# Four heads in one query tile, and projections two heads further ahead, in an attention and mixture-of-experts kernel

## The chip, the cores and the metric

The kernel runs on one core of a Trainium2 chip. The metric is the time of one execution on the device in microseconds (us); lower is better. The median of five runs is given for the kernel before, and one more execution was taken with the hardware profiler. PE is TensorE (matmul), PEld its weight load, DVE is VectorE, ACT ScalarE, POOL GpSimd, SP SyncE, which issues most DMAs. A name with q behind it (SPq) is the queue of that engine.

## What is computed

The input x is 4 sequences of 512 tokens with 256 features, all in float32. Reduced to what matters:

```python
xn = layernorm(x)                                  # over 256 features
q, k, v = xn @ Wq, xn @ Wk, xn @ Wv                # 16 query heads, 4 key/value heads, 128 wide
q, k = rotate(q) * xs, rotate(k) / xs              # rotary embedding with a position scale
s = softmax(causal(q @ k.T / sqrt(128))) @ v @ Wo  # query heads 4m .. 4m+3 share k and v head m
y = sum over the 2 best of 16 experts of weight * (silu(xn @ Wg) * (xn @ Wu)) @ Wd
y = y + (silu(xn @ Sg) * (xn @ Su)) @ Sd           # the shared expert, 352 wide
out = x + s * silu(y)
```

Causal means that query token t sees only the keys of tokens 0 to t of its sequence.

## The kernel before

There are G = 64 heads in all: 4 sequences of 16. One loop (L1038) runs over steps g, and each step works on several heads at different stages: it projects head g (`project`, L709), makes the scores and the exponentials of head g-2 (`score`, L734; `exponents`, L761), turns the probabilities of head g-3 (`turned`, `sent`, `brought`, L807 to L831), multiplies those of head g-4 by the values (`weigh`, L833), and makes a quarter of an output projection for the group of four heads that ended two groups ago (`output`, L857). The order on PE, DVE, ACT and SP is the order in which the program is written (`manual_schedule`, L1025); POOL's order is left to the tool that schedules the program.

**Projection.** A head is two matmuls of 128x128 weights with 512 tokens (L690) into a PSUM tile `pr` (two buffers). ACT copies the two halves crosswise (L698, L699), DVE multiplies and adds (L702, L704, L706). With every fourth head comes a key head, projected in the same way, in the step where g % 4 is 0. Each head has a tile qT of its own, with three buffers.

**Scores.** A query tile is 128 consecutive tokens of one head, so a head has four, i = 0 to 3. Tile i needs the first (i+1)*128 keys: one matmul of 128, 256, 384 or 512 columns (L753). DVE adds the mask and finds the maximum (L756), ACT takes the exponential and sums (L766). The four results stand side by side in a tile `prob` of 1280 columns (two buffers), and `normalise` (L777) multiplies by 1/sum on ACT (L783).

**Turning.** The weighted sum needs the probabilities transposed. For heads below GT = 61, DVE transposes blocks of 32x32 in five instructions (`turned`, L814). `sent` writes the result to DRAM with four DMAs on SP's queue (pt_d, L827), and `brought` reads it back in another order (pT, L831). SP works through its queue in order and waits in it. The last three heads are transposed by TensorE.

**Weighing and output.** `weigh` (L847) makes four matmuls of 512, 384, 256 and 128 columns into `po`, and ACT copies the result into a tile oT (L853). `output` multiplies a token tile of four heads by Wo (L863) and adds to s_sb.

**Plain steps.** `plain(g)` (L655) names steps with little beside attention. In them `output` comes ahead of `weigh` and `normalise` stands ahead of both; in other steps the order is `weigh`, `normalise`, `output`. PSUM banks of scores are also chosen by it.

**Everything else** is put at named places of steps (`put`, L920, six places in each step: START, SCORED, TURNED, PROJECTED, WEIGHED, END): the value projections (`value`, steps 0 to 2 for the first sequence and 6 to 10 for the others), the shared expert (`shared_hidden`, L567, three pieces of eight matmul passes for each sequence; `shared_down`), the router (steps 6 to 18), the scatter of tokens into blocks by indirect DMAs on POOL (steps 16 to 23, four in each), 40 blocks of expert work (steps 24 to 46: `block_load` with a copy `wb` on POOL, `block_hidden`, `block_down`), gathers and the final gate (from step 46). The statistics of later sequences are made by ACT (`stats_of`, L264) and POOL (`stats_of_last`, L278), and POOL normalises them (L300). DMAs in the list `later` are issued once a step, just after `brought`: among them clearing xs_d and ys_d (L178), weights, and from step 52 on writing s_d and reading it back (sr, L634).

Of the kernel before, what the change touches and what calls it, by code (L numbers as in the profile page):

```python
# [12 lines left out]
F32 = mybir.dt.float32  # L13
# [15 lines left out]
def kernel(  # L29
# [14 lines left out]
):  # L44

# [127 lines left out]
    nc.sync.dma_start(rp[:, :2], rope[:2].rearrange("k p s -> p k s"))  # L173
    for b in range(1, B):
        nc.sync.dma_start(xn[:, ts(b, NQ), :], xf[:, ts(b, NQ), :])
# [6 lines left out]

    def load_rest():
        nc.sync.dma_start(sgu, sh_gate_up.rearrange("(c p) j -> p c j", p=P))
        load_wq(1)
# [25 lines left out]
    )  # L211
    eps_t = const.tile([P, 1], F32, name="eps_t")
# [124 lines left out]
    both = rt.tile(full, F32, name="r_both")  # L337
# [52 lines left out]
    def route_slots():  # L390

        nc.gpsimd.tensor_sub(pos, run, both)

        cn = ps_s.tile([P, 2, E], F32, name="s")
        nc.tensor.matmul(cn[:, 0, :], before, run[:, NT - 1, :], start=True, stop=True)
        nc.tensor.matmul(cn[:, 1, :], ones, run[:, NT - 1, :], start=True, stop=True)
        cnt = rt.tile([P, 2, E], F32, name="r_cnt")
        nc.scalar.copy(cnt, cn)
        yield

        sq = [P, E, NT]
        cmp = rt.tile(sq, F32, name="r_cmp")
        nc.vector.tensor_tensor(
            cmp, cnt[:, 1, :].unsqueeze(2).to_broadcast(sq),
            steps.unsqueeze(1).to_broadcast(sq), ALU.is_gt,
        )
        nb = rt.tile([P, E], F32, name="r_nb")
        nc.vector.tensor_reduce(nb, cmp, AX.X, ALU.add)
        yield
        cum = rt.tile([P, E, E], F32, name="r_cum")  # L410
        nc.vector.tensor_tensor(
            cum, nb.unsqueeze(1).to_broadcast([P, E, E]), upto, ALU.mult
        )
        end = rt.tile([P, E], F32, name="r_end")
        nc.vector.tensor_reduce(end, cum, AX.X, ALU.add)
        yield
        base = rt.tile([P, E], F32, name="r_base")
        nc.vector.tensor_sub(base, end, nb)
        nc.vector.scalar_tensor_tensor(
            base, base, float(P), cnt[:, 0, :], ALU.mult, ALU.add  # L420
        )
        nc.gpsimd.tensor_tensor(pos, pos, base.unsqueeze(1).to_broadcast(full), ALU.add)
        for k in range(K):
            nc.gpsimd.tensor_mul(pick[k], pick[k], pos)
        yield
        sf = rt.tile([P, K, NT], F32, name="r_sf")
        for k in range(K):
            nc.vector.tensor_reduce(sf[:, k, :], pick[k], AX.X, ALU.add)
        nc.vector.tensor_copy(slot, sf)
        yield  # L430

        wide = [1, NB, E]
        le = rt.tile(wide, F32, name="r_le")
        nc.vector.tensor_tensor(
            le, iota_b.unsqueeze(2).to_broadcast(wide),
            end[0:1, :].unsqueeze(1).to_broadcast(wide), ALU.is_ge,
        )
        yield
        ex = rt.tile([1, NB], F32, name="r_ex")
        nc.vector.tensor_reduce(ex, le, AX.X, ALU.add)  # L440
        nc.vector.tensor_scalar_min(ex, ex, float(E - 1))
        nc.vector.tensor_copy(blk[:, :NB], ex)
        nc.vector.tensor_copy(blk[:, NB:], end[0:1, E - 1 :])
# [28 lines left out]
    def block_xs(i, n):  # L472

        xs = fe.tile([P, 2, D], F32, name="xs")
        nc.sync.dma_start(xs[:, :n, :], xs_d[i * P : (i + n) * P, :].rearrange("(n p) d -> p n d", p=P))
        for k in range(n):
            xsT_t[i + k] = xs[:, k, :]

    def block_load(i, copy=nc.gpsimd.tensor_copy):
# [7 lines left out]
        wb = fe.tile([P, NC, 2 * IB], F32, name="wb", bufs=3)  # L487
# [44 lines left out]
    def block_down(i, n):  # L532
# [5 lines left out]
        if not ys_t:  # L538
            ys_t.append([fe.tile([P, 2, D], F32, name="ys"), 0])
# [27 lines left out]
    def shared_hidden(b, c):  # L567

        if c == 0:
            hsT_t[b] = w2.tile([P, NS, S], F32, name="hsT")  # L570
# [83 lines left out]

    def plain(g):  # L655


        return g % GRP and (ROUTED <= g < E0 or E1 + 2 * NS <= g < GT + 2)

# [26 lines left out]
    def rotated(b, w, h, cs, sn, name, bufs):  # L686
# [14 lines left out]
        r = w2.tile([P, S], F32, name=name, bufs=bufs)  # L701
# [4 lines left out]
        nc.vector.tensor_add(r, pr, t2)  # L706
        yield r

    def project(g):  # L709

        b, h = divmod(g, NH)
        if h % GRP == 0:
            for kT[b, h // GRP] in rotated(b, wk, h // GRP, 2, 3, "kT", 2):
                yield
        for qT[g] in rotated(b, wq, h, 0, 1, "qT", 3):
            yield
# [16 lines left out]

    def score(g, i):  # L734


        b, h = divmod(g, NH)
        if i == 0:
            last = g == G - 1
            pb = w2.tile([P, off[NQ]], F32, name="turned" if last else "prob", bufs=2)  # L740
            mx = small.tile([P, NQ], F32, name="mx")
            prob[g] = (pb, mx)
        pb, mx = prob[g]
        w = (i + 1) * P
# [5 lines left out]
        elif i == NQ - 1 and g < GT and not E0 < g + 2 < E1:  # L750
# [3 lines left out]
            sc[:, :w], qT[g][:, ts(i, P)], kT[b, h // GRP][:, :w], start=True, stop=True  # L754
        )
        nc.vector.tensor_tensor_reduce(  # L756
            pb[:, off[i] : off[i + 1]], sc[:, :w], mask[:, S - w :],
# [3 lines left out]
    def exponents(g, i):  # L761
# [3 lines left out]
        pi = pb[:, off[i] : off[i + 1]]  # L765
# [11 lines left out]
    def normalise(g, i):  # L777
# [3 lines left out]
        pi = pb[:, off[i] : off[i + 1]]  # L781
# [51 lines left out]
    def weigh(g):  # L833
# [16 lines left out]
        oT[g] = w2.tile([P, S], F32, name="oT", bufs=2 * GRP)  # L850
        if g < GT:
            po = po.rearrange("p (a i q) -> p i a q", a=QB, q=32)
            paced.append(nc.scalar.copy(oT[g].rearrange("p (i a q) -> p i a q", a=QB, q=32), po))  # L853
        else:
            paced.append(nc.scalar.copy(oT[g], po))

    def output(q, t, pool=ps_s, name="s"):  # L857
# [4 lines left out]
        for j in range(GRP):  # L862
            nc.tensor.matmul(  # L863
                s, oT[q * GRP + j][:, ts(t, P)], wo[:, k * GRP + j, :],
# [13 lines left out]
    def ending(j, t):  # L878

        h = NH - GRP + j  # L880
        if j == 0:
# [3 lines left out]
            end_t[t], oT[G - GRP + j][:, ts(t, P)], wo[:, h, :],  # L885
# [10 lines left out]
    def weigh_last():  # L896
# [5 lines left out]
        oT[g] = w2.tile([P, S], F32, name="oT", bufs=2 * GRP)  # L902
        for t in range(NQ + 1):
            if t < NQ:
# [6 lines left out]
                nc.scalar.copy(oT[g][:, ts(t, P)], po[:, ts(t, P)])  # L911
# [15 lines left out]
    ROUTED = NH - 1  # L927

    put(0, TURNED, router_weights)
    put(0, PROJECTED, value, 0, 0, PO, PS)  # L930
    put(1, PROJECTED, value, 0, 1, TP, TP)
    put(1, PROJECTED, value, 0, 2, PO, PS)
    put(2, PROJECTED, value, 0, 3, TP, TP)

    put(0, START, stats_of_last)
    for n, g in enumerate((0, 0, 0, 0, 1, 1, 2, 3)):
# [13 lines left out]
    for g, f in (  # L950
        (4, partial(load_wo, 0)), (5, partial(load_wq, 2)), (8, partial(load_wo, 1)), (9, partial(load_wq, 3)),
# [10 lines left out]
    for g, p in (  # L962
        (13, PROJECTED), (14, TURNED), (14, TURNED), (15, TURNED), (16, TURNED), (17, TURNED), (18, TURNED)
# [22 lines left out]
    for i in range(1, NB0, 2):  # L986
        g = E0 + 1 + i // 2
        put(g, WEIGHED, block_hidden, i, *(PR if g % GRP else TP))

    for b in range(B):  # L990
        S0 = (3, 12)[b] if b < B // 2 else E1 + NS * (b - B // 2)
        S1 = ROUTED + NQ + 2 * b if b < B // 2 else S0 + NS
# [32 lines left out]
    with tc.manual_schedule(engines={ET.PE, ET.DVE, ET.Activation, ET.SP}):  # L1025
# [11 lines left out]
        load_rest()  # L1037
        for g in range(G + GRP):  # L1038
# [7 lines left out]
            pieces = project(g) if g < G else iter(())  # L1046
# [29 lines left out]
            for _ in range(1 if g % GRP else 2):  # L1076
# [85 lines left out]
```

## Time and profile before

| | us |
|---|---|
| median of 5 runs (743.87 to 746.73) | 745.44 |
| the profiled execution | 747.31 |
| its span, first to last instruction | 745.6 |
| DVE, transposes L814 (x305) | 106.3 |
| ACT, exponentials L766 (x252) | 140.2 |
| ACT, normalise L783 (x246) | 118.4 |
| PE, projections L690 (queries, x256) | 121.2 |
| PE, weigh L847 (x504) | 147.4 |
| PE, output L863 (x472) | 111.7 |

The span is what lies between the first and the last instruction; the execution's own time is 1.7 us longer. Busy times of an engine are sums over its instructions. Those of PE overlap, as a matmul is still in the pipeline when the next one starts, so the means of single matmuls are longer than the distance between two starts. DMAs moved 154.87 MB, a mean of 208 GB/s; the 61 reads pT have a median of 4.4 us from issue to landing, the 244 writes pt_d 2.8 us. An "x" behind a group is its count.

### The profile page before, as it was taken

What the parts mean: (1) busy time and instruction counts of PE and PEld (TensorE: products, weight loads), DVE (VectorE), ACT (ScalarE), POOL (GpSimd) and SP (SyncE); (2) the same over time, 40 slices, a digit from 0 to 9 for tenths busy, and PEclk for the clock granted to TensorE, in tenths of its full rate; (3) what the DMA queues carried; (4) which work ended last, traced back from release to release, by engine and by line L of the source; (5) the groups of instructions that cost most, each with busy time, mean ns of one, the idle gap of its engine ahead of it and who ended that gap; (6) DMA issues with size and microseconds to landing.
All of it is one profiled execution on the core that took longest, in us unless ns stands there. A gap on an engine that the chain in (4) does not pass through costs nothing. (4 is left out here: it accounts for less than half of the span.)

```text
span 745.6 us, 10635 instructions
## 1 busy us (share of the span) xinstructions
PE 730.6 (98%) x2990; PEld 496.0 (67%) x2990; DVE 518.3 (70%) x1558; ACT 495.1 (66%) x1262; POOL 139.5 (19%) x203
## 2 busy tenths in 40 slices
PE   8989999999999999999999999999999999989997
PEld 5546676565766677777777777777556566656676
DVE  4575678878676767675766757666675769978752
ACT  4987766657676766666576666666565758767752
POOL 2730000004542200000000000000342255710000
PEclk9999999999999999999999999999999999999999
DMA  9157688766866888787779788783664565876610
GB/s 302 56 170 220 197 250 280 237 202 192 238 215 182 273 249 255 219 269 224 235 235 301 237 243 274 214 259 113 189 206 145 161 185 178 258 210 195 178 35 29
DMA packets 100213, 154.87 MB, mean 208 GB/s; under 512 B 9288, under 2 KB 80056, under 8 KB 100152
## 3 DMA queue, kind: packets, MB, share of 16 engines
q1 hardware_dynamic: 96792, 145.51, 64.3%
q0 software_dynamic: 3072, 8.39, 3.4%
q8 instruction: 25, 0.41, 0.2%
q14 instruction: 36, 0.29, 0.1%
q10 hardware_dynamic: 288, 0.26, 0.1%
HBM read 90.72 MB, written 63.41 MB: 207 GB/s over the span
## 5 line engine op out<-in xcount | busy, mean ns | idle before, releaser
L766 ACT ACTIVATE prob<-prob,mx 128x128 f32<-128x128 f32 x252 | 140.2, 557 | 24.0 <-DVE mx L756 17.2
L847 PE MATMUL po<-pT,v_sb 128*128 128x512 f32 x504 | 147.4, 436 | 3.1 <-ACT prob L783 2.1
L847 PEld LDWEIGHTS po<-pT,v_sb 128*128 128x128 f32 x504 | 94.6, 191 | 67.1 <-issue 39.9
L756 DVE CUSTOM_DVE_ANT_0 prob<-sc,mask 128x512 f32<-128x512 f32 (+3 forms) x151 | 77.8, 518 | 78.0 <-PE sc L753 73.8
L783 ACT ACTIVATE prob<-prob,ri 128x512 f32<-128x512 f32 x246 | 118.4, 553 | 11.3 <-DVE ri L774 10.8
L690 PE MATMUL pr<-xnT,wq 128*128 128x512 f32 x256 | 121.2, 596 | 1.4 <-DVE kT L706 1.4
L814 DVE STREAM_TRANSPOSE turned<-prob 128x384 f32<-128x384 f32 x305 | 106.3, 409 | 10.1 <-ACT prob L783 10.0
L863 PE MATMUL s<-wo,oT 128*128 128x256 f32 x472 | 111.7, 379 | 0.9 <-PEq L557 0.9
L753 PE MATMUL sc<-kT,qT 128*128 128x384 f32 (+3 forms) x310 | 105.8, 456 | 0.1
L863 PEld LDWEIGHTS s<-wo,oT 128*128 128x128 f32 x472 | 86.4, 190 | 17.9 <-issue 8.3
L698 ACT COPY rot<-pr 64x512 f32<-64x512 f32 x80 | 46.6, 582 | 51.9 <-PE pr L690 51.7
L853 ACT COPY oT<-po 128x512 f32<-128x512 f32 x61 | 35.6, 584 | 62.2 <-PE po L847 62.2
L690 PEld LDWEIGHTS pr<-xnT,wq 128*128 128x128 f32 x256 | 47.6, 192 | 39.0 <-issue 35.1
L702 DVE TENSOR_TENSOR rot<-rot,rp 128x512 f32<-128x512 f32 x80 | 55.9, 699 | 10.4 <-ACT rot L699 9.6
L488 POOL COPY wb<-wg 128x256 f32<-128x256 f32 x40 | 16.1, 403 | 241.0 <-DMA wg<-in_L_ffn_w_gate_up_dram 212.1
L753 PEld LDWEIGHTS sc<-kT,qT 128*128 128x128 f32 x310 | 53.2, 190 | 11.2 <-DVE mx L756 2.0
L704 DVE TENSOR_TENSOR pr<-pr,rp 128x512 f32<-128x512 f32 x80 | 54.9, 686 | 0.3
L597 POOL DMA_INDIRECT yk<-ys_d,slot x32 | 32.7, 1021 | 78.9 <-DVE xn L605 46.5
L766 ACT ACTIVATION_READ_ACCUMULATOR prob<-prob,mx 128x1 f32 x252 | 47.1, 187 | 0.0
L699 ACT COPY rot<-pr 64x512 f32<-64x512 f32 x80 | 46.2, 577 | 1.0
L706 DVE TENSOR_TENSOR qT<-pr,rot 128x512 f32<-128x512 f32 x64 | 44.2, 691 | 2.2
L575 PE MATMUL tp<-xnT,sgu 128*118 128x512 f32 (+1 forms) x96 | 43.2, 593 | 0.9 <-DVE hsT L469 0.9
(202 smaller groups left out, 960.8 us busy)
## 6 DMA issues: line engine op xcount, KB each, us to landing
pt_d<-turned SPq DMA_DIRECT2D x244, 160.0 KB, 2.8
pT<-pt_d SPq DMA_DIRECT2D x61, 640.0 KB, 4.4
wg<-in_L_ffn_w_gate_up_dram SPq DMA_DIRECT2D x40, 352.0 KB, 4.1
wd<-in_L_ffn_w_down_dram SPq DMA_DIRECT2D x40, 256.0 KB, 4.4
xs_d<-zero SPq DMA_DIRECT2D x7, 768.0 KB, 6.5
xs<-xs_d SPq DMA_DIRECT2D x20, 256.0 KB, 6.4
ys_d<-ys SPq DMA_DIRECT2D x20, 256.0 KB, 3.0
v_d<-v_st SPq DMA_DIRECT2D x12, 264.0 KB, 3.0
```

What stands on the lines that cost most here:

```text
L690: nc.tensor.matmul(pr, w[:, c, ts(h, HD)], xnT[:, c, ts(b, S)], start=(c == 0), stop=(c == NC - 1),)
L698: nc.scalar.copy(t2[:hh], pr[hh:])
L699: nc.scalar.copy(t2[hh:], pr[:hh])
L702: nc.vector.tensor_mul(t2, t2, rp[:, sn, :])
L704: nc.vector.tensor_mul(pr, pr, rp[:, cs, :])
L753: nc.tensor.matmul(sc[:, :w], qT[g][:, ts(i, P)], kT[b, h // GRP][:, :w], start=True, stop=True)
L756: nc.vector.tensor_tensor_reduce(pb[:, off[i] : off[i + 1]], sc[:, :w], mask[:, S - w :], -SCALE, HIGHEST, ALU.add, ALU.min, mx[:, i : i + 1],
L766: nc.scalar.activation(pi, pi, AF.Exp, bias=mx[:, i : i + 1], scale=-1.0, accum_out=sums_t[g][:, i : i + 1],)
L783: nc.scalar.activation(pi, pi, AF.Copy, scale=ri[:, i : i + 1])
L814: nc.vector.transpose(bT_t[g][:, :, a : a + d * (len(js) - 1) + 1 : d, :].rearrange("p m j q -> p j m q"), pb[:, off[i] + js[0] * P : off[ ...
L847: nc.tensor.matmul(o, v_sb[b][:, j, k, lo : lo + HD], r, start=(j == 0), stop=(j == NQ - 1))
L863: nc.tensor.matmul(s, oT[q * GRP + j][:, ts(t, P)], wo[:, k * GRP + j, :], start=(j == 0), stop=(j == GRP - 1),)
```

## The change

**Query tiles.** For the first 15 groups of four heads (heads 0 to 59) a query tile no longer holds 128 tokens of one head, but 32 tokens (a unit, QU = 32) of each of the four heads of a group. A group has 16 such tiles, and the step that handled head 4m+k now handles tiles k, 4+k, 8+k and 12+k. Tile 4i+k ends with token 128i + 32(k+1) - 1, so its scores, mask, exponentials and normalisation go to `width` = 128i + 32(k+1) columns instead of 128(i+1). The rest of the last 128-column block has to be zero for the transposes: the two `prob` buffers become fixed tiles, cleared at the start, and for k = 0 and 1 POOL clears 64 columns behind each of the four pieces (from the second group on). A second mask, `mask4`, serves these tiles. The last group keeps the old tiles.

**qT and oT** become tiles of four heads with two buffers each. The rotation's last add (L706 before) writes runs of 32 columns into qT; the copy of `po` (L853) writes runs of 32 into oT, where the four heads again lie apart.

**Order.** All four heads of a group have to be projected before its first score, so step g projects head g+2 (`AHEAD`); the loop starts at step -2, and steps 62 and 63 project nothing. The key head comes in steps where (g+2) % 4 is 0 (`keys`). Values of the first sequence, early statistics and loads of weights move with it: wq(1) and the shared expert's weights are loaded ahead of x of the later sequences, and the statistics move by one step. `plain` now covers steps 15 to 19 instead of 15 to 23 and excludes key steps. The hidden part of the shared expert of the second sequence moves from steps 12 to 14 to steps 20 to 22, its second part from 21 to 23; that of the first begins in step 2 instead of 3.

**Memory.** xs, ys and hsT have one buffer instead of two, wb two instead of three; some router tiles share memory with others.

```diff
+    nc.sync.dma_start(sgu, sh_gate_up.rearrange("(c p) j -> p c j", p=P))
+    load_wq(1)
     for b in range(1, B):
         nc.sync.dma_start(xn[:, ts(b, NQ), :], xf[:, ts(b, NQ), :])
...
+    QU = P // GRP
+    mask4 = wat.tile([P, S], F32, name="mask4")
...
-        xs = fe.tile([P, 2, D], F32, name="xs")
+        xs = fe.tile([P, 2, D], F32, name="xs", bufs=1)
...
-        wb = fe.tile([P, NC, 2 * IB], F32, name="wb", bufs=3)
+        wb = fe.tile([P, NC, 2 * IB], F32, name="wb", bufs=2)
...
+    AHEAD = 2
+
+    def keys(g):
+
+        return (g + AHEAD) % GRP == 0 and g + AHEAD < G
+
     def plain(g):
-        return g % GRP and (ROUTED <= g < E0 or E1 + 2 * NS <= g < GT + 2)
+        return not keys(g) and (ROUTED <= g < S1_0 + 1 or E1 + 2 * NS <= g < GT + 2)
...
     def project(g):
         b, h = divmod(g, NH)
         if h % GRP == 0:
-            for kT[b, h // GRP] in rotated(b, wk, h // GRP, 2, 3, "kT", 2):
-                yield
-        for qT[g] in rotated(b, wq, h, 0, 1, "qT", 3):
-            yield
+            kT[b, h // GRP] = w2.tile([P, S], F32, name="kT")
+            yield from rotated(b, wk, h // GRP, 2, 3, kT[b, h // GRP])
+
+            qT[g // GRP] = w2.tile([P, GRP * S], F32, name="qT")
+        j, q = g % GRP, qT[g // GRP]
+        if g < G - GRP:
+            q = q.rearrange("p (b h q) -> p b h q", h=GRP, q=QU)[:, :, j, :]
+        else:
+            q = q[:, ts(j, S)]
+        yield from rotated(b, wq, h, 0, 1, q)
...
+    prob_t = [w2.tile([P, off[NQ]], F32, name=f"prob{k}", bufs=1) for k in range(2)]
+    for pb in prob_t:
+        nc.gpsimd.memset(pb, 0.0)
+
+    def width(g, i):
+
+        return i * P + (g % GRP + 1) * QU if g < G - GRP else (i + 1) * P
...
+            elif GRP <= g < G - GRP and k < 2:
+
+                for j in range(1, NQ + 1):
+                    lo = off[j] - P + (k + 1) * QU
+                    nc.gpsimd.memset(pb[:, lo : lo + 2 * QU], 0.0)
...
-        w = (i + 1) * P
+        w = width(g, i)
...
-            sc[:, :w], qT[g][:, ts(i, P)], kT[b, h // GRP][:, :w], start=True, stop=True
+            sc[:, :w], qT[q][:, ts(i * GRP + k if g < G - GRP else k * NQ + i, P)],
+            kT[b, h // GRP][:, :w], start=True, stop=True,
...
-        pi = pb[:, off[i] : off[i + 1]]
+        pi = pb[:, off[i] : off[i] + width(g, i)]
...
-        if g < GT:
-            po = po.rearrange("p (a i q) -> p i a q", a=QB, q=32)
-            paced.append(nc.scalar.copy(oT[g].rearrange("p (i a q) -> p i a q", a=QB, q=32), po))
+        if g < G - GRP:
+            o = oT[q].rearrange("p (b k q) -> p b k q", k=GRP, q=QU)[:, :, k, :]
+            po = po.rearrange("p (b q) -> p b q", q=QU)
...
     ROUTED = NH - 1
+    S1_0 = ROUTED + NQ
...
-    for n, g in enumerate((0, 0, 0, 0, 1, 1, 2, 3)):
+    for n, g in enumerate((1, 1, 1, 1, 2, 2, 3, 3)):
         put(g, END, stats_of, NQ + n)
...
     for b in range(B):
-        S0 = (3, 12)[b] if b < B // 2 else E1 + NS * (b - B // 2)
-        S1 = ROUTED + NQ + 2 * b if b < B // 2 else S0 + NS
+        S0 = (2, S1_0 + 1)[b] if b < B // 2 else E1 + NS * (b - B // 2)
+        S1 = S1_0 + b * (NS + 1) if b < B // 2 else S0 + NS
...
-        for g in range(G + GRP):
+        for g in range(-AHEAD, G + GRP):
             a, n, w, q = g - 2, g - 3, g - 4, g - 2 * GRP
...
-            pieces = project(g) if g < G else iter(())
+            pieces = project(g + AHEAD) if g + AHEAD < G else iter(())
...
-            for _ in range(1 if g % GRP else 2):
+            for _ in range(2 if keys(g) else 1):
                 next(pieces, None)
```

## The prediction

> **What bounds it now.** I read the engine totals first, then TensorE's groups by shape, then the chain that ended last, then single stretches of the timeline. Totals, span and granted clock, from the page:
>
> ```profile
> span 745.6 us, 10635 instructions
> ...
> PE 730.6 (98%) x2990; PEld 496.0 (67%) x2990; DVE 518.3 (70%) x1558; ACT 495.1 (66%) x1262; POOL 139.5 (19%) x203
> ...
> PEclk9999999999999999999999999999999999999999
> ```
>
> A busy TensorE need not be a full one, so I checked the chain of waits in late steps (start, length, what):
>
> ```profile
> 698.37 1.73 PE s L863 x8
> 700.09 2.16 PE po L847 x8
> 702.25 1.72 PE pr L690 x4
> 703.97 2.38 PE sc L753 x8
> 706.35 2.16 PE po L847 x8
> ```
>
> Each piece begins where the last ends, and length follows columns: 4 passes of 512 in 1.72, 8 of 256 in 1.73, so 0.84 ns a column and pass (every f32 matmul is two passes: 80 projections of two chunks give 320 records). Added up over all 2990 records by columns this is 716 us. About 19 us are holes: some 10 before 80 us, 2.3 at 665, 1.1 at 525, 0.8 at 178. So a column removed from TensorE shortens the span at its place, unless what TensorE waits for there is not shortened.
>
> **Scores, columns removed.** Heads 0 to 59 are 15 groups of four. Head k of a group now multiplies 128i + 32(k+1) keys instead of 128(i+1). Shapes before:
>
> ```profile
> L753 PE MATMUL sc<-kT,qT 128*128 128x384 f32 x128 | 51.9, 487 | 0.1
> ...
> L753 PE MATMUL po<-kT,qT 128*128 128x128 f32 x82 | 15.9, 275 | 0.2 <-ACT v_sb L675 0.2
> ```
>
> The means contain the pipeline's latency; starts of successive passes lie 0.109, 0.216, 0.322 and 0.429 us apart at 128, 256, 384 and 512. For i = 1 to 3 a group saves (96+64+32) columns x 3 tiles x 2 passes x 0.838 ns = 0.965 us; 15 groups: 14.5 us. For i = 0 the weight load can set the pace. The only narrow passes are the router's of 16 columns:
>
> ```profile
> 148.08 0.29 PE L395 MATMUL s<-r_run,before 128*128 128x16 f32 x2
> 148.22 0.38 PE L396 MATMUL s<-r_run,ones 128*128 128x16 f32 x2
> 148.45 1.10 PE L847 MATMUL po<-pT,v_sb 128*128 128x512 f32 x2
> ```
>
> Their starts are 28, 112, 112 and 111 ns apart: the first follows a wide pass with its partner's load early, then one load takes about 112. A pair of 32 columns costs 28 + 112 = 140 ns instead of 218, one of 64 the same, one of 96 162, one of 128 all 218: 78+78+56 = 0.21 us a group, 3.2 us in all. Sum **-17.7 us**; ends 14.5 and 17.7. The two moved projections (3.43 us of TensorE) and the third shared_hidden are moved, not removed.
>
> **DVE and ACT** lose the same columns in L756, L766 and L783 (ACT: 402 ns at 128, 721 at 512). Both have room (about 6.2 and 5.9 us of a 7.76 us step), so I count nothing. The rotation's add and the oT copy get outputs in runs of 32: the transposes L814 write such runs, 553 ns for 384 columns, against 691 for the plain 512-column add. Bounds -0 to +0.2 us per head on DVE, hidden behind 1.5 us of room; taken as 0.
>
> **POOL.** 28 heads get four clears of 128x64. A clear of 128x512 took 0.53 us and of 128x1 0.09, so about 0.15 each by that line, 0.6 us a head; two of 1280 columns, some 1.3 us each, and the second mask lie before 18 us, where POOL waited 13.4 us for x. Each adds a wait: DVE's transposes (L814) need the clears, and behind them DVE's scores wait. On POOL they stand behind the scatter's four indirect DMAs (1.27 us apart), the wb copies (they end at 359.9, the next step begins at 360.9) or a finish. They are wanted only at the next step's start, 7 us on. Taken as 0; bounds 0 and 2 us.
>
> Single buffers for xs, ys and hsT: xs is then loaded after the transposes at 357.4 to 358.0 instead of at 355.9; next on SP's queue is pt_d at 363.35, xs is wanted at 370. wb's second copy waits for the hidden matmuls, which end about when it came anyway. All 0.
>
> **The front.** Up to q2 (ends 21.7) TensorE's order stays. Then q3, value 3 and the second kT follow, to 27.0, and score(0) at 27.2. But four stats_of (1.18 us each) now stand in ACT's queue ahead of that kT's rotation, so its PSUM bank comes free near 36 while TensorE wants it at 33.9; a second hole of 2 us comes at 56, where xn of the second sequence is normalised by POOL. I get the end of weigh(1) at 60.7 against 58.1 before, with 3.4 us more projection done and 1.2 us of scores saved: 60.7 - 3.4 + 1.2 - 58.1 = **+0.4**; ends -1.5 and +5.
>
> **Steps 11 to 16 lose their cover.** weigh(n) needs head n's probabilities turned by DVE, written to DRAM and read back. From the start of turning to landing I read 9.7 us (head 11, 152.95 to 162.6) to 14.7 (head 6, 96.2 to 110.9, beside zeros and wo). Steps 12 to 14 held shared_hidden(1), 3.43 us each, and step 12 a kT; that was the cover. In such a step ACT normalises after weigh, so turning n+2 starts 4.45 us after weigh(n) (136.89 to 141.31). Steps become 7.36, 7.54, 7.76, 8.92 (kT now there), 7.36 us. From step 11 at 0: weigh(8) is reached at 11.0, its data at 11.3; weigh(9) at 19.1 and 20.2; weigh(10) at 29.1 and 30.6; weigh(11) in time. For weigh(12), SP's queue before:
>
> ```profile
> 158.84 0.34 SPq L831 DMA_DIRECT2D pT<-pt_d  x1
> 159.23 2.51 SPq L196 DMA_DIRECT2D sd<-n_L_ffn_shared_down_dram  x3
> 161.78 2.03 SPq L178 DMA_DIRECT2D ys_d<-zero  x1
> 165.92 3.72 SPq L827 DMA_DIRECT2D pt_d<-turned  x4
> 173.23 0.34 SPq L831 DMA_DIRECT2D pT<-pt_d  x1
> ```
>
> The zeros crowd pt_d already, and weigh(12) waited 0.8 us. TensorE now comes some 2.5 us sooner: wait 3.3 with part of a slow clock. Sum 0.3+1.1+1.5+3.3-0.8 = **+5.4**; ends 0 (DMAs keep pace) and 9.
>
> **Step 58.** A reload of s_d stops SP for 3 us, and weigh(54) waits 2.26. From the start of step 56 the data came after 24.9 us; TensorE now needs 7.54+7.76+5.03 = 20.3 to get there instead of 22.8, since kT moves from step 56 to 58: **+2.2**, ends 0 and 4. The 0.5 at weigh(51) goes, as step 54 gains a kT: **-0.5**.
>
> **A long hole costs twice.** Windows around 665 (PE, PEld, DVE, ACT, POOL busy, granted clock, DMA share, GB/s):
>
> ```profile
> 665.00:667.00 2.00, 1.59 (x4) 1.00 (x5) 1.97 (x6) 1.49 (x4) 0.00 (x0) 0.91 0.99 358
> 667.00:670.00 3.00, 3.00 (x7) 1.77 (x7) 0.84 (x3) 0.59 (x1) 0.00 (x0) 0.50 0.45 75
> ```
>
> After 2.26 us of idling the clock stood at 0.5 for 3.4 us, which costs 1.7; holes up to 1.6 did not do it. [...]
>
> **The tail.** Steps 62 and 63 hold no projection. Head 59's data landed 9.6 us after its turning began (693.96 to 703.6); TensorE now reaches weigh(59) 8.4 us after score(60), the data 9.3: **+0.9**; ends 0 and 3.4 (all the moved work leaves holes).
>
> **Sum.** -17.7+0.4+5.4+2.2-0.5+0.9 = -9.3. The profiled execution took 747.3 (span 745.6 and 1.7 around it), so 738.0 by it; it lies 1.9 above the median of 745.44, and for the median I say **736**. All good ends give 726, all bad ones 751.
>
> **Rivals.** *Full gain*: DMAs land sooner where they have less company, the holes in 11 to 16 do not come. For it: head 11's 9.7 us. Against: 265 GB/s at DMA share 0.8 already from 92 to 142 us, and more bytes per time now. 745.4-17.7 = 728. *Given back*: the holes reach 9, 4 and 5 us, with slow clocks; about 744. *Slower*: the DRAM round trip becomes the bound in every light step. In 11 to 19 and 52 to 63, without blocks or hidden work, about 13.1 us lie between turning and weigh; head 13 took 12.85, head 6 14.7. If shorter steps crowd the queue so that it averages 14.5, 14 such steps lose 1.4 us each (20 us) and some five fall to the slow clock (8 us): -17.7+8+28 = +18, about 763. It outweighs the gain from 13.8 us on. Against: heads 57, 59 and 60 took 9.6 to 10.0. *The columns do not shorten TensorE*, as when a pass has a floor above its columns: refuted by 0.109 to 0.429 in step with columns, except for i = 0.
>
> **Chances.** Forecast (732 to 742) 0.50; full gain 0.22; given back (742 to 748) 0.15; slower 0.13. Range 727 to 747: it leaves out the slower case and a few below. 0.3% (2.2 us, to 743.2) is about what a measurement here tells from no change: faster 0.77 (forecast, full gain, a third of given back), within 0.10, slower 0.13.
>
> **What would show it.** Score groups of 32 to 512 columns whose starts follow columns; the TensorE total down by about 17; holes ahead of po at weigh(9) to weigh(12) released by pT, a longer one at weigh(54), each over 2 us with a granted clock of 0.5 behind it; no wait of L814 for POOL. I am wrong if L814 waits for the clears, if weigh waits in every light step, or if the front opens by more than 5 us.

## The result, and the profile after

The changed kernel is slower: 748.12 us median of 52 runs (744.65 to 755.29) against 745.43 of 94 runs of the kernel before (743.31 to 750.01). The ratio is 1.0036, 95% interval 1.0028 to 1.0045, so +2.7 us where -9.3 was worked out. The forecast was 736 us, its range 727 to 747; the measured time lies above the range and on the other side of the kernel before.

Line numbers have moved: scores L753 to L794, `weigh` L847 to L889, output L863 to L911, projections L690 to L708, transposes L814 to L856, pt_d L827 to L869, pT L831 to L873. The page of the kernel after, totals:

```profile
span 747.2 us, 10915 instructions
...
PE 721.3 (97%) x2990; PEld 494.6 (66%) x2990; DVE 510.5 (68%) x1558; ACT 474.9 (64%) x1262; POOL 158.1 (21%) x322
...
PEclk9999999998999999999999999999999999999999
```

TensorE is busy 9.3 us less (721.3 for 730.6; that the forecast was the same number is chance) and the span is 1.6 us longer: work did go, and waiting came. One slice no longer has the full clock. The costliest group names the wait (busy, mean ns | idle before, releaser):

```profile
L889 PE MATMUL po<-pT,v_sb 128*128 128x512 f32 x504 | 148.9, 439 | 14.3 <-DMA pT<-pt_d 12.5
```

Before, the same group idled 3.1 us: 1.0 of it is put down to pT, and 2.1, the hole at head 54, to ACT.

**Where the time went, in the trace.** For each pass of TensorE I took the distance to the next start, less 0.838 ns a column. What is left over, where it is more than 15 ns, is idle time, half clock and a floor under narrow passes: 18.9 us before, 40.2 after. The columns themselves fell by 19.3 us. By place:

| place | forecast, us | from the two traces, us |
|---|---|---|
| columns of the scores, by their starts | -17.7 | -14.3 |
| front, to 80 us | +0.4 | +4.2 |
| steps 11 to 16 | +5.4 | +9.3 |
| heads 53 and 54 (steps 57, 58) and head 51 | +1.7 | -0.1 |
| tail, from head 61's scores | +0.9 | +3.5 |
| elsewhere | 0 | +0.5 |
| the scores' own floor, held in these places too | | -1.1 |
| sum | -9.3 | +2.0 (span +1.6) |

The third column compares one trace with one trace, so it holds each one's luck. In the row of heads 53 and 54 the holes did grow, by 1.4 us with head 51's, but the trace before has a stretch of half clock behind head 54, which costs 1.8 us, and the trace after has none. In the tail's row the hole at head 59 is 2.91 us; in three other traces with the same order there (those of the next section with the hidden products back, with the clear of ys_d late and with the big clears late) it is 1.32 to 1.35.

**Scores.** Head 16 of the kernel after (first of its group, 32 columns in the first tile) in TensorE's timeline: start, length, what.

```profile
193.49 0.30 PE L794 MATMUL tp<-kT,qT 128*128 128x32 f32 x2
193.63 1.00 PE L794 MATMUL sc<-kT,qT 128*128 128x160 f32 x4
194.47 0.86 PE L794 MATMUL s<-kT,qT 128*128 128x416 f32 x2
195.16 1.88 PE L708 MATMUL pr<-xnT,wq 128*128 128x512 f32 x4
```

Start to start the head takes 195.16 - 193.49 = 1.67 us; the third of a group (96 columns first) takes 2.00, the fourth, which is full, 2.15. Heads 0 to 2 of a group save 0.48, 0.32 and 0.16, some 14.3 us in 15 groups. The first pair of 32 does end after 0.14 us, as forecast. But the median distance from the first 160-column pass to the next start is 219 ns, where its columns need 134, and behind every narrow pair it is 218 to 220: what the narrow pair gains, the next pass waits.

**Steps 11 to 16.** SP's queue in the kernel after, then TensorE at head 12's weighted sum, then two stretches of 3.41 us (PE, PEld, DVE, ACT, POOL busy, granted clock, DMA share, GB/s):

```profile
161.05 2.48 SPq L198 DMA_DIRECT2D sd<-n_L_ffn_shared_down_dram  x3
163.57 2.01 SPq L184 DMA_DIRECT2D ys_d<-zero  x1
165.62 5.65 SPq L869 DMA_DIRECT2D pt_d<-turned  x4
175.00 0.34 SPq L873 DMA_DIRECT2D pT<-pt_d  x1
```

```profile
172.45 1.89 PE L911 MATMUL s<-wo,oT 128*128 128x256 f32 x8
179.55 4.60 PE L889 MATMUL po<-pT,v_sb 128*128 128x512 f32 x8 [5.21 <-DMA pT<-pt_d]
```

```profile
173.82:177.24 3.42, 0.52 (x3) 0.12 (x1) 3.35 (x10) 2.13 (x6) 1.88 (x2) 1.00 0.40 82
177.24:180.65 3.41, 1.10 (x2) 0.61 (x3) 0.94 (x3) 0.00 (x0) 2.64 (x7) 0.50 0.98 340
```

The four sends that took 3.72 us on the queue before now take 5.65, pT is issued 1.8 us later than before, and TensorE gets there 2.8 us sooner: it waits 5.2 us, where it had waited 0.67. From 177.24 to 184.06 the clock is 0.50, so the sum itself runs at half speed, 4.60 us for 2.4. Head 9's sum waits 1.55 us, which the profile puts down to a router operation on DVE; its pT had been issued 4.8 us before, so which of the two it waited for is open.

**The tail.** Steps 62 and 63 of the kernel after; before, the three pieces shown in the prediction followed each other without a gap:

```profile
700.06 2.32 PE L889 MATMUL po<-pT,v_sb 128*128 128x512 f32 x8
702.22 2.63 PE L794 MATMUL sc<-kT,qT 128*128 128x128 f32 x8
707.77 2.39 PE L889 MATMUL po<-pT,v_sb 128*128 128x512 f32 x8 [2.91 <-DMA pT<-pt_d]
```

**The clock of the unprofiled runs.** The profiled execution has a mean granted clock of 0.993. Over 54 executions of the changed kernel the median is 0.991 (0.986 to 0.995), over 23 of the kernel before 0.999 (0.997 to 1.000). Time multiplied by what is missing from 1 gives the clock's loss: 6.7 us an execution against 0.7. No single trace shows that.

### The profile page after: what moved, and what is told of

Read it like the earlier page. It is cut to its first block, busy times and chain, and to the rows that moved or that the text cites. A ratio compares the mean times of both kernels' runs of the same rounds, so it can differ in the third digit from the quotient of the medians.

```text
span 747.2 us, 10915 instructions
## 1 busy us (share of the span) xinstructions
PE 721.3 (97%) x2990; PEld 494.6 (66%) x2990; DVE 510.5 (68%) x1558; ACT 474.9 (64%) x1262; POOL 158.1 (21%) x322
## 5 line engine op out<-in xcount | busy, mean ns | idle before, releaser
L889 PE MATMUL po<-pT,v_sb 128*128 128x512 f32 x504 | 148.9, 439 | 14.3 <-DMA pT<-pt_d 12.5
L889 PEld LDWEIGHTS po<-pT,v_sb 128*128 128x128 f32 x504 | 94.9, 192 | 81.1 <-issue 55.2
L808 ACT ACTIVATE prob<-prob,mx 128x128 f32<-128x128 f32 (+3 forms) x252 | 130.4, 518 | 20.1 <-DVE mx L798 17.8
L708 PE MATMUL pr<-xnT,wq 128*128 128x512 f32 x256 | 120.4, 593 | 1.5 <-DVE kT L725 1.5
L798 DVE CUSTOM_DVE_ANT_0 prob<-sc,mask 128x512 f32<-128x512 f32 (+12 forms) x151 | 70.4, 471 | 72.8 <-PE sc L794 70.3
L825 ACT ACTIVATE prob<-prob,ri 128x512 f32<-128x512 f32 (+3 forms) x246 | 108.8, 514 | 12.7 <-DVE ri L816 12.2
L911 PE MATMUL s<-wo,oT 128*128 128x256 f32 x472 | 111.7, 379 | 0.1
L856 DVE STREAM_TRANSPOSE turned<-prob 128x384 f32<-128x384 f32 x305 | 106.3, 409 | 6.7 <-ACT prob L825 6.5
L794 PE MATMUL sc<-kT,qT 128*128 128x384 f32 (+12 forms) x310 | 97.1, 428 | 0.1
L911 PEld LDWEIGHTS s<-wo,oT 128*128 128x128 f32 x472 | 86.2, 190 | 15.5 <-issue 5.7
L708 PEld LDWEIGHTS pr<-xnT,wq 128*128 128x128 f32 x256 | 47.6, 191 | 39.0 <-issue 34.5
L719 DVE TENSOR_TENSOR rot<-rot,rp 128x512 f32<-128x512 f32 x80 | 57.6, 720 | 14.2 <-ACT rot L717 13.5
L794 PEld LDWEIGHTS sc<-kT,qT 128*128 128x128 f32 x310 | 51.6, 190 | 7.8 <-DVE mx L798 2.0
L781 POOL MEMSET prob<- 128x64 f32 x112 | 15.7, 153 | 185.5 <-DVE turned L856 109.2
```

The lines of the kernel that those rows point to most:

```text
L708: nc.tensor.matmul(pr, w[:, c, ts(h, HD)], xnT[:, c, ts(b, S)], start=(c == 0), stop=(c == NC - 1),)
L719: nc.vector.tensor_mul(t2, t2, rp[:, sn, :])
L794: nc.tensor.matmul(sc[:, :w], qT[q][:, ts(i * GRP + k if g < G - GRP else k * NQ + i, P)], kT[b, h // GRP][:, :w], start=True, stop=True,)
L798: nc.vector.tensor_tensor_reduce(pb[:, off[i] : off[i] + w], sc[:, :w], (mask4 if g < G - GRP else mask)[:, S - w :], -SCALE, HIGHEST, ALU ...
L808: nc.scalar.activation(pi, pi, AF.Exp, bias=mx[:, i : i + 1], scale=-1.0, accum_out=sums_t[g][:, i : i + 1],)
L825: nc.scalar.activation(pi, pi, AF.Copy, scale=ri[:, i : i + 1])
```

## The theory and its rivals

**T**: the columns are saved, and the new order gives them back, because pieces of work that stood ahead of waits have moved: it is a sum of lost covers, each with a place. (A cover is work that TensorE does while the data of its next piece are on their way; a hole is its idle time where the cover is too short.) **T2**, beside it: long holes also bring half clock. **R1**: the change's own additions (clears, single buffers, strided writes) cost the time. **R2**: the way of the turned probabilities through DRAM bounds every light step, so that shorter scores can gain little.

## Experiments

Times are medians; the ratio to the kernel before in the same set of runs follows with its interval. Where a variant is compared with the changed kernel or with another variant, the difference is that of the two ratios, times 745.5 us.

### Columns alone

The kernel before, with this:

```diff
+    def width(g, i):
+        return i * P + (g % GRP + 1) * (P // GRP) if g < G - GRP else (i + 1) * P
...
-        w = (i + 1) * P
+        w = width(g, i)
...
-        pi = pb[:, off[i] : off[i + 1]]
+        pi = pb[:, off[i] : off[i] + width(g, i)]
```

The two probability tiles are fixed and cleared once at the start here too, so the big clears are in it; the first key product starts at 9.16 us, where it is 8.72 before and 10.39 in the changed kernel.

> The kernel before, with only the score products, the exponents and the scaling of heads 0 to 59 shortened to the keys that the changed kernel uses; order, projections and buffers stay as before. The head's own tiles stay, so scores beyond the width are left out and the mask does not fit: only the time counts. Theory T (the columns are really saved, 0.96 us a light group by the starts of the score products in the changed kernel's trace, 14.3 us in all, and given back by the moved projections and by cover taken from steps 11 to 16, the front and the tail): 731 to 734 us against 745.4. Rival R1 (the changed kernel's own clears, single buffers and strided writes eat the gain; none of them is here): 728 to 732, the 17.7 us of the prediction. Rival R2 (the way of the turned probabilities through DRAM is the bound of the light steps, so that shorter score products only lengthen the wait of the weighted sums): 740 to 746, with holes before the weighted sums in most steps.

Measured: 733.8 us, 0.984 (0.9826 to 0.9855), so -11.8 us against 745.6 in its own set. T holds and R2 does not; R1, which kept the forecast's 17.7 us, misses by a third of it. The group of weighted sums:

```profile
L855 PE MATMUL po<-pT,v_sb 128*128 128x512 f32 x504 | 148.1, 437 | 5.4 <-DMA pT<-pt_d 5.4
```

The group idles 5.4 us instead of 3.1. At head 12, before and with columns alone:

```profile
177.80 2.39 PE L847 MATMUL po<-pT,v_sb 128*128 128x512 f32 x8 [0.67 <-DMA pT<-pt_d]
```

```profile
175.18 2.39 PE L855 MATMUL po<-pT,v_sb 128*128 128x512 f32 x8 [1.71 <-DMA pT<-pt_d]
```

The holes at heads 12 and 54 exist in the old order too, and shorter scores open them a little. Left-over time of TensorE is 26.6 us against 18.9; 19.3 - 7.7 = 11.6, close to what was measured.

### The order alone

```diff
-        return i * P + (g % GRP + 1) * QU if g < G - GRP else (i + 1) * P
+        return (i + 1) * P
```

> The changed kernel's order, buffers and strided tiles, with every score product, exponent and scaling at the full width of its query tile (and so without the small clears between heads). The mask of the four interleaved heads is kept, so the scores beyond their keys are not those of the reference: only the time counts. It shows what the new order costs with no column saved. Theory T (the order costs what columns alone, 733.8, and the changed kernel, 748.1, are apart, 14.4 us, less what the longer score products cover of the new holes, at most 0.5 us at each of six): 757 to 762 us. Rival R1 (the clears between heads or the shortened products cost the time, the order nothing): 745 to 748.

Measured: 760.2 us, 1.0199 (1.0168 to 1.0231), +15.4 us against 744.8 in its set. With -11.8 for the columns the sum is +3.6, and both together measure +2.7: the two halves add up within a microsecond. There are no clears between heads in it, so R1 falls for these; the big clears, the single buffers and the strided writes are still in it, and the runs below take these up.

### The shared expert's second sequence back in steps 12 to 14

```diff
-        S0 = (2, S1_0 + 1)[b] if b < B // 2 else E1 + NS * (b - B // 2)
-        S1 = S1_0 + b * (NS + 1) if b < B // 2 else S0 + NS
+        S0 = (2, 12)[b] if b < B // 2 else E1 + NS * (b - B // 2)
+        S1 = S1_0 + 2 * b if b < B // 2 else S0 + NS
```

(and with it `plain` to step 23 again, as before, and both sequences' hidden values in one tile)

> The changed kernel with the shared expert's hidden products of sequence 1 back in steps 12 to 14 and their second part back from step 21. Both sequences share one tile of hidden values, so sequence 1 overwrites sequence 0's before these are used up: the output of the shared expert is not the reference's. Theory T (steps 12 to 14 lost the work that covered the wait for the transposed probabilities): the hole of 5.4 us at the weighted sum of head 12 and the two stretches at half clock after it (3.4 us) go, as does most of the 1.7 us at head 9's neighbours: 739 to 742 us against 748.1 for the changed kernel. Rival R1 (clears, single buffers, strided writes): no change, 747 to 749. Rival R2 (DRAM round trip bound in every light step): 746 to 749, since work put in three steps leaves the other steps' waits as they are.

Measured: 739.9 us, 0.9926 (0.9905 to 0.9947): 8.2 us come back by the two ratios. TensorE at head 12:

```profile
180.56 1.89 PE L911 MATMUL s<-wo,oT 128*128 128x256 f32 x8
182.28 2.32 PE L889 MATMUL po<-pT,v_sb 128*128 128x512 f32 x8
```

No hole, full speed. From head 8's sum to head 13's the left-over time is 0.7 us, where it was 10.7 in the changed kernel. The strided tiles, single buffers (hsT apart) and clears are all still there, so this step is over half of what the order costs (8.2 of 15.4 us).

### The clear of ys_d six steps later

```diff
-        (14, load_last),
+        (14, load_last), (20, partial(zeros, ys_d, NB0, NB)),
```

(with `zeros(ys_d, NB0, NB)` taken out of `load_last`)

> The changed kernel with the clear of the second DRAM buffer of the experts (896 KB of zeros, six of the other DMAs' size) sent at step 20 instead of step 14. Theory T in its narrow form (the hole of 5.4 us at the weighted sum of head 12 comes from the queue: its transposed probabilities wait for their turn behind and beside this traffic): 741 to 744 us against 748.1, hole at head 12 under 2 us and full clock after it. If the hole comes from the thin cover of steps 12 to 14 alone, and the DMA's traffic has no part in it: 747 to 749, hole unchanged. Rival R1 (clears, single buffers, strided writes): 747 to 749, hole unchanged.

Measured: 745.8 us, 1.0008 (0.9987 to 1.0030), some 2.1 us better and short of the forecast; the interval just touches the changed kernel's. SP's queue, then TensorE at head 12:

```profile
163.42 3.52 SPq L867 DMA_DIRECT2D pt_d<-turned  x4
172.24 0.35 SPq L871 DMA_DIRECT2D pT<-pt_d  x1
```

```profile
176.92 2.39 PE L887 MATMUL po<-pT,v_sb 128*128 128x512 f32 x8 [2.93 <-DMA pT<-pt_d]
```

The sends take 3.52 us again, pT is issued 2.8 us sooner than in the changed kernel, and the hole ahead of the sum shrinks from 5.21 to 2.93 us, and the sum takes 2.39 us instead of 4.60. So 2.3 us of it were the crowded queue; the rest goes with the missing work, as the experiment before shows.

### The big clears behind the first transposes

```diff
+            turned_first = copy(xnT[:, c, :S], tps[c])
+        late_clears(turned_first)   # mask4, then the two prob tiles of 1280 columns
```

> The changed kernel with the set-up of the second mask and the two clears of the whole probability tiles (1280 columns each) on GpSimd held back until the last copy of the first transposes is made. Theory T (the front's 4.2 us come in part from these clears, beside which VectorE's normalisation of the first rows took 1.89 and 1.46 us instead of 0.73 each, and from the half clock that follows the later start of the transposes): 744.5 to 746.5 us against 748.1; the first key product starts at 8.7 us instead of 10.4. If VectorE's slow normalisation has another cause (the rows' arrival, the table load on ScalarE): 747.5 to 748.5, the normalisation still over 1.4 us.

Measured: 746.5 us, 1.0010 (0.9992 to 1.0028), some 1.9 us better, at the edge of T's range; the interval touches the changed kernel's, and TensorE's left-over time up to 80 us falls by the same 1.9 us. The timeline of POOL in the changed kernel, then that of DVE, which normalises the first rows beside it:

```profile
5.96 1.15 POOL L762 MEMSET prob<- 128x1280 f32 x1
...
7.57 1.30 POOL L762 MEMSET prob<- 128x1280 f32 x1
```

```profile
5.87 1.89 DVE L270 TENSOR_SCALAR xn<-xn,mv,rstd 128x256 f32<-128x256 f32 x2
...
7.87 1.46 DVE L270 TENSOR_SCALAR xn<-xn,mv,rstd 128x256 f32<-128x256 f32 x2
```

and DVE with the clears held back:

```profile
6.65 0.73 DVE L274 TENSOR_SCALAR xn<-xn,mv,rstd 128x256 f32<-128x256 f32 x2
```

The pairs return from 1.89 and 1.46 us to 0.73 each, and the first key product starts at 8.44 instead of 10.39. So the clears beside them, and not the rows' arrival or the table load, had slowed DVE. Each slow pair runs beside a clear (5.87 to 7.76 us beside 5.96 to 7.11, and 7.87 to 9.33 beside 7.57 to 8.87); by what the one slows the other, the rows do not show.

### Tail and combinations

First the last four heads' projections spread over steps 58 to 62, keys at 58, query of head g+1 in step g:

```diff
+            elif g + AHEAD == G - GRP:
+                pieces = project(G - GRP, "keys")
+            else:
+                pieces = project(g + 1, "query") if g + 1 < G else iter(())
```

> The changed kernel with the projections of the last four heads spread: the keys at step 58, the queries one step ahead (heads 60 to 63 at steps 59 to 62) instead of two (58 to 61). Theory T (the tail lost the projections that stood ahead of the weighted sum of head 59, which waits 3.1 us in the profiled execution and 1.5 to 1.9 us in three others): that hole falls under 0.5 us, the time by 1.5 to 3 us, to 745 to 746.6. If the hole is set by the transfers alone and moves with them: 747.5 to 749.

Measured: 751.5 us, 1.0074 (1.0049 to 1.0098): 2.8 us worse, a miss. The hole at head 59 did go. But head 60's query had stood ahead of the weighted sum of head 54. TensorE in this kernel there:

```profile
667.37 0.86 PE L797 MATMUL s<-kT,qT 128*128 128x416 f32 x2
671.03 3.71 PE L892 MATMUL po<-pT,v_sb 128*128 128x512 f32 x8 [2.80 <-DMA pT<-pt_d]
```

and in the changed kernel:

```profile
664.89 1.88 PE L708 MATMUL pr<-xnT,wq 128*128 128x512 f32 x4
669.42 2.39 PE L889 MATMUL po<-pT,v_sb 128*128 128x512 f32 x8 [2.65 <-DMA pT<-pt_d]
```

The 1.88 us of projection are gone, and the sum runs slower (3.71 us for 2.39). The hole is hardly longer, since TensorE had been slowed on the way as well: head 53's sum, at 660.75 behind a hole of 2.10 us, took 3.67 us where it takes 2.40 in the changed kernel, and the projection behind it 2.34 for 1.88. The changed kernel's trace has a granted clock of 1.00 from 184.06 to its end. All six executions had a clock of 0.989. A cover was taken from one hole to fill another. Why head 53's hole, which the edit does not touch, was 2.10 us here and 1.18 in the changed kernel's trace, is not shown.

Then the covers together: the shared expert's hidden values back in steps 12 to 14, in memory of the router's that is free by then; the clear of ys_d at step 20; the big clears late; and this tail.

```diff
+                two = rt.tile([P, 2, S], F32, name="wv")
+                hsT_t[b] = [two[:, 0], two[:, 1], rt.tile([P, S], F32, name="v_st", bufs=2)]
```

> The changed kernel with four steps of its order mended: the shared expert's hidden products of sequence 1 at steps 12 to 14 in buffers that the router's part of the memory has free by then (the values' weights and staging), the clear of the second DRAM buffer at step 20, the set-up clears of GpSimd behind the first transposes, and the last four heads' queries one step ahead. Theory T (the loss is a sum of lost covers, each with its hole): 8.2 us by the experiment with the hidden products (which holds most of the 2.3 us by the later clear of DRAM), 1.6 by the late clears, 1.5 to 3 by the tail: 735 to 738 us against 748.1, granted clock 0.995 or more. If the covers only move the waits on: 740 to 744.

Measured: 739.5 us, 0.9916 (0.9892 to 0.9940), above T's range of 735 to 738: the tail's part of it was the miss above, whose result came in the same set of runs. The next kernel also has, in the front,

```diff
-    put(4, PROJECTED, norms)
+    put(4, WEIGHED, deviations)
+    put(4, WEIGHED, norms)
...
-            put(4 + b, (PROJECTED, WEIGHED)[c], turn, b, c)
+            put(4 + b, ((WEIGHED, END) if b == 1 else (PROJECTED, WEIGHED))[c], turn, b, c)
```

> The last kernel, and in the front the square root of the row deviations (with its table load of 1.28 us on ScalarE) and the normalisation behind the weighted sum of step 4 instead of ahead of it, and the transposes of sequence 1 one place later. Theory T (the hole of 2.3 us at the score product of head 3 is the copy of the weighted sum, queued on ScalarE behind that table load): the hole falls by 1.5 us or more, and with it the risk of half clock: 1 to 3 us below the last kernel, 733 to 736. If the bank is free no sooner, or the later normalisation on GpSimd makes the transposes wait as long: within 1 us of the last kernel.

Measured: 740.9 us, 0.9928 (0.9902 to 0.9955), no gain. The hole at head 3's scores fell from 2.3 to 0.7 us as T had it, but a wait, put down to DVE, stands one piece on, and the sum behind it runs slower (4.12 us for 2.32):

```profile
60.08 4.12 PE L898 MATMUL po<-pT,v_sb 128*128 128x512 f32 x8 [2.56 <-DVE mx L807]
```

Last, the covers with another tail: head 60's query stays at step 58, head 61's at 59, heads 62 and 63 go to steps 61 and 62.

```diff
+            p = g + AHEAD if g + AHEAD < G - 2 else g + 1
+            pieces = project(p) if p < G and g != G - 4 else iter(())
```

> The kernel that keeps the covers, with the last four heads spread otherwise: the keys and head 60's query stay at step 58 and head 61's at step 59 as in the changed kernel, heads 62 and 63 go to steps 61 and 62. Theory T (spreading them before had taken 1.88 us of products from the front of the weighted sum of head 54, which waits anyway): the two holes at heads 53 and 54 return to 3.8 us together, the hole at head 59 stays under 1.5, and the time falls by 1.5 to 3 us, to 736.5 to 738. If the hole at head 54 depends on the transfers alone: 739 to 740.

Measured: 736.5 us, 0.9868 (0.9846 to 0.9889), as T had it. It beats both kernels, by 1.3% and 1.7%, and the holes at heads 53 and 54 are 1.17 and 2.61 us. TensorE at head 59:

```profile
695.30 2.32 PE L895 MATMUL po<-pT,v_sb 128*128 128x512 f32 x8
```

It starts as the scores ahead of it end. These are the same columns and clears as in the changed kernel, and the same tiles but for one sequence's hidden values; it is 12.5 us faster, by the places of its work. Columns alone in the old order are still 2.1 us faster, about as much as the hole of 2.3 us that is left in the front; that this is all of it was not tried. So what R1 can have cost, by the small clears, the single buffers and the strided writes together, is of that size at most, unless the new places gain something that the old ones did not.

### The clock

```diff
+        for _ in range({9: 3, 12: 10, 53: 2, 54: 5, 59: 3}.get(g, 0)):
+            nc.tensor.matmul(po[:, :D], zero[:, :P], zero, start=True, stop=True)
```

> The changed kernel with products of zeros (128x256, two passes, some 0.43 us each) ahead of the weighted sums that wait, into the bank that the sum then overwrites: 3 at head 9, 10 at head 12, 2 at head 53, 5 at head 54, 3 at head 59, each less than the hole it stands in. No wait is shortened by it. Theory T2 (beside the holes themselves the changed kernel loses the half clock that follows them: its executions show a mean granted clock of 0.991 at the median against 0.999 before, 6.7 us against 0.7): the clock rises to 0.995 to 0.997, what is left being the front's, and the time falls by 3 to 5 us, to 743 to 745. If the lower clock has another cause (the load of the whole kernel, the chip): clock unchanged, 748 to 750.

Measured: clock 0.997 at the median (0.994 to 1.000), as T2 had it; time 745.6 us, 0.9999 (0.9986 to 1.0012), some 2.8 us better, a little short of T2's range. At head 12 the granted clock stays 1.00 and

```profile
173.91 4.48 PE L881 MATMUL po<-zero 128*128 128x256 f32 x20
179.43 2.42 PE L891 MATMUL po<-pT,v_sb 128*128 128x512 f32 x8 [1.03 <-DMA pT<-pt_d]
```

the sum starts at 179.43, as before, and takes 2.42 us instead of 4.60. So the lower clock does come from the holes (0.991 at the median with them open, 0.997 with the zeros in them). It gave 4.5 us of the clock's loss back and 2.8 of the time: where TensorE is slow on its way to the next wait, that wait is shorter, and some of the zeros outlast their hole. How much each is, the runs don't tell.

> The last kernel, with 2 products of zeros ahead of the weighted sum of head 53 and 5 ahead of head 54's. Theory T2 (half clock after the holes): its clock rises by 0.002 or more over the last kernel's, and the time falls by 1.5 to 3.5 us, to 734 to 736. If the clock has another cause, or the two stretches do not fall on these holes: the time of the last kernel within 1 us.

(The kernel of 736.5 us with the same lines for `{53: 2, 54: 5}`.) Measured: 737.0 us, 0.9884 (0.9861 to 0.9906). The clock rose from 0.997 to 0.999, as T2 had it, and the time did not fall, which T2 had wrong: here the zeros gain nothing. That they cost what they save is likely and not shown.

## Why the prediction was wrong

The mechanism was for the most part the forecast's: work is removed from TensorE, and covers that the new order takes away give it back, at the places named. The sizes failed on both sides. The columns bring 11.8 us, not 17.7 (5.9 short); the order costs 15.4, not 8.4 (7.0 more); the two halves overlap by 0.9; 12.0 in all, from -9.3 to +2.7. Two steps failed most: the price of the narrow passes, and the wait at head 12 with the half clock behind it. The big clears, at nothing in the sum, are a third.

- **"A pair of 32 columns costs 28 + 112 = 140 ns instead of 218"** failed. By its starts the pair does cost 140, and the pass behind it gives the gain back: 29 + 111 + 220 ns for the pair and a pass of 160 columns, which is two of 112 and the 136 of the 160 columns. So a pass of 32 columns cost what one of 128 does. The router's row in the trace before says the same: the pass of 512 columns at 148.45, behind the four narrow ones, takes 513 ns to the next start instead of 429. The prediction read up to that pass and not past it. It had its own bound of 14.5, which is nearer the 14.3 measured from the starts. Another 2.5 us are lost elsewhere, a part of it in holes that shorter steps opened in the old order as well (head 12: 0.67 to 1.71 us).
- **Front, "+0.4"**: 4.2, inside its bound of 5, but 2.9 of it lies ahead of 20 us. What had been priced at nothing there was "two of 1280 columns, some 1.3 us each": the price of the clear was right (1.15 and 1.30 us), but what it delayed was not POOL's own queue, it was DVE beside it, and a stretch of half clock followed (0.50 from 9.98 to 13.40 us). The two holes of 2 us came (1.5 at 37 us, 2.3 at 57), the second put down to ACT's copy of a weighted sum and not to POOL's normalisation; the order before had holes there too, so the stretch from 20 to 80 us is only 1.3 us worse.
- **Steps 11 to 16, "+5.4"**: 9.3. The working put 1.1, 1.5 and 3.3 us at heads 9, 10 and 12; the holes are 1.55, 0.25 and 5.2. At head 12 the sends, crowded by ys_d's zeros, took 1.9 us longer than before, and the prediction had kept their old times; without the zeros the hole is 2.93, near its 3.3. The two stretches of half clock behind it cost 3.4 us and were counted as "part of a slow clock".
- **Step 58, "+2.2", and head 51, "-0.5"**: -0.1 in the table, by luck of the traces. The data of head 54 came when forecast, 24.7 us after the start of step 56. TensorE needed 22 us to get there, not 20.3, as it had waited 1.2 us at head 53 on the way, which the forecast did not have. The sum's own numbers give 2.5 rather than 2.2 (22.8 - 20.3). The holes of heads 51, 53 and 54 together grew by 1.4 us, near the 1.7 forecast; the half clock that followed the hole before (0.50 from 666.65 to 670.07) did not follow this one (1.00).
- **Tail, "+0.9"**: 3.5 in the trace. TensorE came when forecast, 8.5 us after head 60's scores; the data took 11.8 us from the start of turning instead of the 9.6 read off before. In the three other traces named above the hole is less than half as long; why the data took so long in this one is open.
- **Half clock**: "holes up to 1.6 did not do it" and a hole of 2.26 did. It was priced for one hole of a single trace. Over the executions the clock loses 6.7 us against 0.7, of which the zeros' experiment brought back 2.8 in time: the one thing here that no single trace could show.
- The waits for POOL's 112 small clears at nothing: right (no instruction in the trace waited for L781). The single buffers and the strided writes at nothing: not refuted; the kernel of 736.5 us has them too, hsT apart, and lies 2.1 us from columns alone.
- Of the rivals, *given back* came nearest (losses of 9.3, 4.2 and 3.5 us, with slow clocks), with a chance of 0.15; it said about 744, as it kept the full gain of the columns. *DRAM bound in every light step* was refuted by columns alone.

## What to carry to other kernels

When a change moves work, list every wait that the work stood ahead of, and price each with the transfer's time as it will be then, in its new company on the queue, not as it was. Try the gain and the reordering as two kernels: here -11.8 and +15.4 lay behind +2.7. And before filling a hole from elsewhere, look at what the filler was covering there.

## What the runs showed of the hardware

**Half clock followed windows that were 62% idle or more.** In the traces of the kernel before and of the one after, the granted clock changes on a grid of 3.41 us: between the first and the last change in each, its stretches are 3.41, 6.83, 75.09, 163.84 and 563.20 us long, which is 1, 2, 22, 48 and 165 times 3.413. From 20 us after the start to 20 us before the end, three windows of that grid were followed by a clock of 0.50: the records leave TensorE idle for 62% of the one from 663.24 before, 85% of the one from 173.82 after, and 68% of the next, from 177.24, which ran at 0.50 itself. No window in which TensorE is idle for 58% or less was. Two windows that differ by little, in the kernel before and in the one after:

```profile
663.24:666.65 3.41, 1.31 (x4) 0.68 (x4) 3.34 (x9) 1.92 (x4) 0.00 (x0) 1.00 0.97 346
666.65:670.07 3.42, 3.42 (x8) 2.09 (x7) 1.19 (x5) 0.59 (x1) 0.00 (x0) 0.50 0.46 91
```

```profile
665.34:668.75 3.41, 1.43 (x4) 0.36 (x2) 3.38 (x9) 2.40 (x8) 0.00 (x0) 1.00 0.81 206
668.75:672.17 3.42, 2.75 (x11) 1.94 (x12) 2.30 (x4) 0.32 (x1) 0.00 (x0) 1.00 0.72 260
```

1.31 us busy of 3.41 (62% idle) brings 0.50; 1.43 (58%) keeps 1.00, though its hole is the longer one (2.65 against 2.10 us): it lies across two windows. What follows for other holes is an estimate from these rows (2.10 us idle of 3.41 do it, 1.98 do not), which takes some 2.0 us within one window as enough: a hole of 2.0 us can then cost 1.7 us more, by chance, and one of 4 us always does. A hole of h us between them falls wholly enough into a window with a chance of 1 - (4.0 - h)/3.41, if where the grid stands against the kernel is chance (it begins 1.05 us after the first instruction in the trace before and 3.16 in the one after): 0.44 for the 2.1 us of the kernel before, 0.75 us on the mean, and its clock does lose some 0.7 (a clock given to 0.001 is a loss given to 0.7 us). In the front of the kernel after, a window that is less idle by the records (46%: 1.84 us busy of 3.40, from 6.60) was followed by 0.50 too; why is not shown.

**A narrow f32 pass handed its gain to the next one.** In the trace after, behind a pair of 32, 64 or 96 columns the next pass took 218 to 220 ns, whether it had 160, 192 or 224 columns. With the pair this makes two passes of 112 ns and the next pass's own columns, so a pass of fewer than 128 columns cost as much as one of 128.
